# Decoder layer on one core: the normalized tokens of the self attention turned by way of memory and VectorE instead of by TensorE

## The chip, the core and the metric

One core of a Trainium2 chip runs the whole layer as one program. Time is microseconds of the device from start to end. The kernel before was run three times (3795.72, 3797.68 and 3800.22 us; the median is 3797.68), and once more with the hardware profiler, which gave the profile that all durations below come from.

## What is computed

The input is 32 sequences (called batches here) of 128 tokens with 512 channels, in fp32. Three blocks follow one another, each as `x = x + block(layernorm(x))`: a differential self attention, a cross attention and a mixture of experts. The change touches the first:

```python
h = (x - mean) / sqrt(var + 1e-5)            # per token
q, k, v = h @ Wq * 0.25, h @ Wk, h @ Wv      # 32 half heads of 16, 16 value heads of 32
aw = softmax(q @ k.T + causal)               # per half head
attn = (aw[0] - lam * aw[1]) @ v             # the two half heads of one head
attn = 0.2 * attn-normalized per head        # (1 - LAMBDA_INIT)
x = x + attn @ Wo
```

`h @ W` sums over channels, and TensorE sums over partitions. A batch arrives with tokens on the partitions, so `h` has to be turned (channels on the partitions, four chunks of 128) before it can be multiplied. How it is turned is what is changed.

## The kernel before, in words

`self_attention` runs over 64 steps, two for each batch `b`: step `n = 2b + cp` works on half `cp` of the channels of `q` and `k` (16 half heads). The work of one step is spread over several turns of the loop in lines 478 to 524 (the first lines of the loop are in `at`: the step that came `ago` turns earlier). Turn `n` issues, in this order: `turn_maxima` and half of the exponentials with their sums (`sums`, L278, ScalarE) for the step before; `maxima` for its own step (scores L251 on TensorE, mask L257 and row maxima L264 on VectorE); `queries_and_keys` (L220) for the next pair of batches, a quarter in each turn; `exponentials` (L308, L315, L318) and the other half of `sums` for the step before; `weigh` (L333, L337, L339) for the step two before; and then either `values` of the next pair (L238, odd turns) or `leave`, the product with Wo (L405, even turns).

Batches go in pairs (`G = 2`): projections are made for a pair, and `hT[g]` holds the turned tokens of pair `g`. Four turns of the loop make up a pair. The tokens of pair `g + 2` are prepared while the attention of pair `g` runs: `measure` (L56 to L66, mean and 1/deviation) in even turns, and in the odd turn behind it `normalize` (L87 on ScalarE: one pass over 128x512), `turn_in` and `load`, which asks for the next batch but one (L151).

`turn_in` is four transposes on TensorE into a PSUM tile (`turn4`, L95) and a copy of that tile by ScalarE into `hT` (L207). The loop calls it for batches 4 to 31, 28 in all; batches 0 to 3 are turned before the loop.

Two things set the order around this. The engines' queues: each engine runs its instructions in the order that the scheduler gave them (outside of the blocks under `manual_schedule`, where the program order holds; `issue_after` puts instructions behind a given one on its engine). And PSUM: every product asks for a tile of two banks from one pool of four (`banks`, `bufs=4`), so that the fourth request after one gets its tile again and has to wait until the earlier one was read out. A turn of the loop makes eight such requests, in program order `turn_maxima`, `maxima` (two), `queries_and_keys`, `exponentials` (two), `weigh`, and `values` or `leave`; an odd turn with `turn_in` makes a ninth.

After the first pair is under way the stage overlaps at its end with the cross attention (`beside`, from turn 60).

Of the kernel before, what the change touches and what calls it, by code (L numbers as in the profile page):

```python
# [10 lines left out]
F32 = mybir.dt.float32  # L11
# [7 lines left out]
P = 128  # L19
E = 512  # L20
EC = E // P
# [14 lines left out]
class Common:  # L36
# [49 lines left out]

        self.nc.scalar.activation(out, src, AF.Identity, bias=down, scale=rstd)  # L87

    def turn4(self, src, order=range(EC)):


        tr = self.banks()[:, 0, :].rearrange("p (c x) -> p c x", c=EC)
        cols = src.rearrange("p (c x) -> p c x", c=EC)
        for c, n in enumerate(order):
            self.nc.tensor.transpose(tr[:, c, :], cols[:, n, :], self.ident)  # L95
        return tr
# [15 lines left out]
            call(*args)  # L112


def self_attention(cm, x, x1_d, Wq, Wk, Wv, Wo, lq1, lk1, lq2, lk2, heads, heads_in, beside):

# [11 lines left out]
    nc, tc, bank = cm.nc, cm.tc, cm.banks  # L130
    B = x.shape[0]
    H, D, G = 16, 32, 2
    CP = 2
    ROW = (16, 0)
    with ExitStack() as ctx:
# [7 lines left out]
        pj2 = early.enter_context(tc.tile_pool(name="a_pj2", bufs=2))  # L143

        xin, xres = {}, {}

        def load(b, queue=nc.sync):

            if b < B:
                xin[b] = pj2.tile([P, E], F32, name="xin")  # L150
                queue.dma_start(out=xin[b], in_=x[b])  # L151
# [10 lines left out]
        for b in range(G):  # L162
            load(b, both[b % 2])
        w = {
            name: (wp if name == "wo" else pj).tile([P, EC, E], F32, name=name)
            for name in ("wk", "wq", "wv", "wo")
        }
        for oc in range(EC):
            for name, src, queue in (("wk", Wk, nc.sync), ("wq", Wq, both[oc < 2])):
                queue.dma_start(  # L170
                    out=w[name][:, :, ts(oc, P)],
                    in_=src[:, ts(oc, P)].rearrange("(c p) m -> p c m", p=P),
                )
            if oc == 0:
                nc.sync.dma_start(out=heads, in_=heads_in)
        vecs = wp.tile([P, 4, 16], F32, name="lam_vecs")
        for i, src in enumerate((lq1, lq2, lk1, lk2)):
            nc.sync.dma_start(out=vecs[:, i, :], in_=src.partition_broadcast(P))
        for name, src in (("wv", Wv), ("wo", Wo)):
            nc.sync.dma_start(out=w[name], in_=src.rearrange("(c p) m -> p c m", p=P))  # L180

        begun = wp.tile([P, 1], F32, name="a_begun")
        nc.scalar.activation(begun, cm.mhalf[:, 0:1], AF.Exp)
# [1 line left out]
        hT, qT, kz, k1, vs = {}, {}, {}, {}, {}  # L185
        last, last_v = {}, [None]
        h, sc_of, qm, expd, u, o, an = {}, {}, {}, {}, {}, {}, {}

        def measure(b):
            if b < B:  # L190
                h[b] = cm.moments(pj2, xin[b], "a_")

        def normalize(b):
            if b < B:
                rstd, down = h[b]
                h[b] = pj2.tile([P, E], F32, name="h")
                cm.shifted(h[b], xin.pop(b), rstd, down)

        def turn_in(b):

            if b >= B:
                return
            g, i = divmod(b, G)
            if i == 0:
                hT[g] = pj2.tile([P, EC, G * P], F32, name="hT")
            tr = cm.turn4(h.pop(b))
            nc.scalar.copy(hT[g][:, :, ts(i, P)], tr)  # L207

        def queries_and_keys(g, oc):

# [220 lines left out]
        for b in range(G):  # L431
# [8 lines left out]
            out=causal, in_=causal, compare_op=ALU.is_ge, fill=NEG, base=0,  # L440
# [32 lines left out]
        for b in range(G):  # L473
            turn_in(G + b)
            load(2 * G + b)
        first.close()
        steps = [(b, cp) for b in range(B) for cp in range(EC // CP)]
        for n in range(len(steps) + 5):
            g, k = divmod(n, 2 * G)
            if n == len(steps) - 2 * G:  # L480
                early.close()
            at = {ago: steps[n - ago] for ago in range(6) if 0 <= n - ago < len(steps)}
            if 1 in at:
                turn_maxima(*at[1])
                sums(*at[1], 0)
            if 0 in at:
                maxima(*at[0])
            queries_and_keys(g + 1, k)
            if 1 in at:
                exponentials(*at[1])  # L490
                sums(*at[1], 1)
            if 2 in at:
                weigh(*at[2])
            if k % 2:
                values(g + 1, k // 2)
            elif 5 in at:
                leave(at[5][0])
            if 2 in at:
                divide(*at[2])
                if at[2][1]:  # L500
                    finish(at[2][0])

            def behind():

                return tc.issue_after(last[at[0]].ins) if 0 in at else nullcontext()

            b = (g + 2) * G + k // 2
            if k % 2 == 0:
                if 3 in at:
                    with behind():  # L510
                        norms(at[3][0])
                measure(b)
                if 4 in at:
                    load_again(at[4][0])
            else:
                normalize(b)
                turn_in(b)
                load(b + G)
                if 4 in at:
                    with behind():  # L520
                        scale_out(at[4][0])
                    turn_out(at[4][0])
            if n in beside:
                beside[n]()


class CrossAttention:
# [101 lines left out]
    def load(self, b):  # L629
        src = self.src  # L630
        src[b, "k"] = self.pi.tile([P, E], F32, name="cx")
        self.nc.sync.dma_start(out=src[b, "k"], in_=self.ctx_in[b])
        src[b, "q"] = self.pi.tile([P, E], F32, name="h2")
        self.nc.sync.dma_start(out=src[b, "q"], in_=self.x1_d[b])

    def measure(self, b):
        q = self.sided[b, "q", 0] = self.pi.tile([P, E], F32, name="xq0", bufs=2)
        self.scale[b] = self.cm.moments_by_sums(self.pi, self.src[b, "q"], q, "x_")
# [575 lines left out]
class Shared:  # L1214
# [4 lines left out]
    G = 4  # L1219
# [482 lines left out]
def decoder_kernel(  # L1702
# [5 lines left out]
    nc = tc.nc  # L1708
# [15 lines left out]
    half_eid = const.tile([P, 2], I32, name="half_eid")  # L1724

    x1_d = dram.tile([B, P, E], F32, name="x1_d")
    h3_d = dram.tile([T, E], F32, name="h3_d")
    h3T_d = dram.tile([B, P, EC, P], F32, name="h3T_d")
    table_ds = [dram.tile([(NX * B + 2) * P, 2], F32, name=f"table_d{i}") for i in range(2)]
# [6 lines left out]
    with tc.tile_pool(name="x_w", bufs=1, side="right") as x_w:  # L1736
        rest = x_w.tile([P, E], F32, name="rest")
        nc.gpsimd.memset(rest, 0.0)
        routing = Routing(cm, x_w, table_ds, B)
        cross = CrossAttention(cm, x_w, x1_d, x2_d, h3_d, h3T_d, ctx_in, routing)  # L1740
        cross.plan(lambda: s_w.load(), lambda: shared.load(0))
        x_ctx = ExitStack()

        def begin():
            cross.begin(
                x_ctx.enter_context(
                    tc.tile_pool(name="x_in", bufs=2, side="right", reuse_waits="tile")
                )
            )
            cross.advance(7)  # L1750

        n = 2 * B
        beside = {
            12: lambda: cross.load_weights(
                xWq, xbq, xWk, xbk, xWv, xbv, xWo, xbo, cos, sin, rotT, gate_w
            ),
            20: lambda: cross.prepare(heads),
            28: routing.prepare,
            n - 4: begin,
        }  # L1760

        for i, count in enumerate((4, 4, 5, 2, 2, 2, 2)):
            beside[n - 3 + i] = lambda count=count: cross.advance(count)
        self_attention(cm, x, x1_d, aWq, aWk, aWv, aWo, lq1, lk1, lq2, lk2, heads, heads_in, beside)
        s_w_pool = ctx.enter_context(tc.tile_pool(name="s_w", bufs=1, reuse_waits="tile"))
        s_w = SharedWeights(cm, s_w_pool, sw_gate, sw_up, sw_down)
        s_h_pool = ctx.enter_context(tc.tile_pool(name="s_h", bufs=2, reuse_waits="tile"))
        shared = Shared(cm, s_h_pool, h3T_d, sum_d, out)
        x_out = ExitStack()
        p2 = x_out.enter_context(tc.tile_pool(name="x_p2", bufs=2, reuse_waits="tile"))  # L1770
        cross.run(p2)
        x_ctx.close()
        s_pool = x_out.enter_context(tc.tile_pool(name="s_p", bufs=1, reuse_waits="tile"))
        shared.use(s_pool, s_w)
        en = mybir.EngineType
        in_order = {en.PE, en.DVE, en.Activation, en.Pool}
        todo = [lambda: cross.rest(2)] * 34 + [
            lambda: routing.tiles(eid, fresh, rows, used, usual, mixed),
            lambda: routing.halves(half, half_eid),
            lambda: nc.sync.dma_start(out=sum_d[T : T + P, :], in_=rest),  # L1780
        ]

        def between():
            if todo:
                todo.pop(0)()

        EARLY = 3  # L1790
        with tc.manual_schedule(engines=in_order):
            for g in range(EARLY - 1):
                shared.group(g, False, between)
            while todo:
                between()
# [103 lines left out]
```

## Time and profile before

| | us |
|---|---|
| three runs, median (lowest to highest) | 3797.68 (3795.72 to 3800.22) |
| the profiled execution | 3800.08 |
| its span, from first to last instruction | 3798.3 |
| TensorE busy in the span | 3717.0 |
| VectorE, ScalarE, GpSimd busy | 2677.8, 2076.4, 1917.2 |
| from 104.37 to 652.9 us, the steady part of the self attention (548.53 us): TensorE, ScalarE, VectorE, GpSimd busy | 547.11, 497.91, 457.85, 282.95 |
| mean granted TensorE clock, share of full | 0.992 |

The self attention has about the first 790 us of the span, the last 75 of them beside the cross attention. In the profile PE is the matmul side of TensorE, PEld its weight loads, DVE VectorE, ACT ScalarE, POOL GpSimd and SPq the queue of SyncE, which issues nearly all of the DMAs. A row of the timeline has the start, the duration, the engine, the line of the kernel, the operation with output and inputs, and in brackets the idle time before it with what ended it. A row with `x16` merges sixteen instructions.

### The profile page before, as it was taken

Reading aid. Unit: us, or ns where it says so; the run is one execution under the profiler, and the core shown is the slowest. Engines: PE = TensorE matmul, PEld = TensorE weight load, DVE = VectorE, ACT = ScalarE, POOL = GpSimd, SP = SyncE. Lnnn points to the kernel's source line nnn. Section 1 sums busy time; section 2 is a strip of 40 time slices with the busy share of each in tenths; the row PEclk is TensorE's granted clock in tenths of the full one; section 3 lists DMA queues with packets and bytes.
Section 4 is the critical chain, followed back from the end, with each engine's and each line's share of the span. In section 5 each row is a group of like instructions: output and inputs, shape, how many; then the busy total and the mean of one; then the engine's idle time right before and its main releaser. Section 6 shows DMA issues by size and latency. Waiting matters only on the chain. (4 is left out here: it accounts for less than half of the span.)

```text
span 3798.3 us, 59896 instructions
## 1 busy us (share of the span) xinstructions
PE 3717.0 (98%) x19060; PEld 1967.8 (52%) x19060; DVE 2677.8 (70%) x5402; ACT 2076.4 (55%) x5616; POOL 1917.2 (50%) x2154
## 2 busy tenths in 40 slices
PE   8999999899999999999999999999999999999999
PEld 5666666534444444444445555555555555555444
DVE  4888888877777778787326777777777777776111
ACT  6989998847677676776402444444444444443000
POOL 3555455545777777777424554555555555553000
PEclk9999999999999999999999999999999999999999
DMA  3111110121221111111135565656566665564210
GB/s 113 34 35 35 35 37 30 39 83 49 62 60 42 51 51 51 48 49 40 56 110 169 128 164 134 166 121 164 122 156 142 150 150 141 135 172 81 89 56 33
DMA packets 146548, 340.25 MB, mean 90 GB/s; under 512 B 28976, under 2 KB 33776, under 8 KB 146160
## 3 DMA queue, kind: packets, MB, share of 16 engines
q1 hardware_dynamic: 89408, 227.75, 18.8%
q0 software_dynamic: 55616, 107.79, 15.4%
q8 instruction: 154, 2.52, 0.3%
q14 instruction: 170, 1.39, 0.1%
q10 hardware_dynamic: 1200, 0.79, 0.1%
HBM read 574.59 MB, written 102.17 MB: 178 GB/s over the span
## 5 line engine op out<-in xcount | busy, mean ns | idle before, releaser
L694 DVE TENSOR_REDUCE nm<-ps 128x2 f32<-128x1024 f32 x512 | 610.6, 1214 | 113.2 <-PE ps L690 106.8
L717 ACT ACTIVATE xp<-ps 128x1024 f32<-128x1024 f32 x512 | 505.8, 1021 | 264.5 <-PE ps L690 202.7
L1644 POOL DMA_INDIRECT sum_d<-e_out,e_into x192 | 309.9, 1614 | 562.6 <-ACT e_out L1641 438.4
L713 PE MATMUL ps<-xqn,xk 32*128 32x512 f32 x2048 | 528.9, 621 | 20.7 <-ACT xp L717 19.1
L1637 PE MATMUL ps<-wd,e_guT 128*128 128x512 f32 (+1 forms) x1152 | 526.9, 593 | 0.3 <-ACT e_guT L1627 0.3
L690 PE MATMUL ps<-xk,xq 32*128 32x512 f32 x2048 | 526.9, 631 | 0.1
L1584 DVE STREAM_TRANSPOSE e_xT<-e_xr 64x256 f32<-64x256 f32 x800 | 499.5, 624 | 18.9 <-DMA e_xr<-h_d,e_run_of 10.7
L1609 DVE STREAM_TRANSPOSE e_guT<-e_gu 32x96 f32<-32x96 f32 x1600 | 477.7, 299 | 25.2
L1569 POOL DMA_INDIRECT e_xr<-h_d,e_run_of x400 | 413.8, 1035 | 159.7 <-issue 150.0
L1598 PE MATMUL ps<-wg,e_xT 128*128 128x352 f32 x1536 | 486.7, 459 | 0.0
L1598 PE MATMUL ps<-wu,e_xT 128*128 128x352 f32 x1536 | 485.7, 459 | 0.0
L1627 ACT COPY e_guT<-e_turned 32x96 f32<-32x96 f32 (+1 forms) x1600 | 407.1, 254 | 25.1 <-DVE e_turned L1620 3.9
L1598 PEld LDWEIGHTS ps<-wg,e_xT 128*128 128x128 f32 x1536 | 289.7, 189 | 217.8 <-issue 94.5
L278 ACT ACTIVATE s<-s,a_nm 128x128 f32<-128x128 f32 x1024 | 395.7, 396 | 5.2 <-DVE a_nm L264 5.2
L1598 PEld LDWEIGHTS ps<-wu,e_xT 128*128 128x128 f32 x1536 | 291.8, 190 | 162.6
L1641 ACT ACTIVATE e_out<-ps,e_weight 128x512 f32<-128x512 f32 x200 | 137.4, 687 | 411.8 <-PE ps L1637 409.5
L1637 PEld LDWEIGHTS ps<-wd,e_guT 128*128 128x128 f32 (+1 forms) x1152 | 218.5, 190 | 228.2 <-issue 188.5
L1602 ACT ACTIVATE e_act<-ps 128x352 f32<-128x352 f32 x200 | 92.6, 463 | 412.7 <-PE ps L1598 412.7
L713 PEld LDWEIGHTS ps<-xqn,xk 32*128 32x128 f32 x2048 | 169.0, 184 | 285.5 <-ACT xp L717 124.5
L1603 DVE TENSOR_TENSOR e_gu<-e_act,ps 128x352 f32<-128x352 f32 x200 | 104.1, 521 | 274.6 <-ACT e_act L1602 274.1
L728 PE MATMUL ps<-xp,v 128*32 128x512 f32 x2048 | 233.0, 595 | 7.9 <-ACT xp L717 7.9
L1031 POOL DMA_INDIRECT table_d<-entry,at x192 | 202.4, 1054 | 64.0 <-issue 52.9
(310 smaller groups left out, 5575.4 us busy)
## 6 DMA issues: line engine op xcount, KB each, us to landing
wg<-in_L_ffn_w_gate_dram SPq DMA_DIRECT2D x192, 704.0 KB
wu<-in_L_ffn_w_up_dram SPq DMA_DIRECT2D x192, 704.0 KB
wd<-in_L_ffn_w_down_dram SPq DMA_DIRECT2D x192, 576.0 KB
wd<-in_L_ffn_w_down_dram SPq DMA_DIRECT2D x192, 128.0 KB
xg<-in_L_ffn_w_gate_dram SPq DMA_DIRECT2D x16, 704.0 KB
xu<-in_L_ffn_w_up_dram SPq DMA_DIRECT2D x16, 704.0 KB
xd<-in_L_ffn_w_down_dram SPq DMA_DIRECT2D x16, 576.0 KB
xres<-in_x_dram SPq DMA_DIRECT2D x32, 256.0 KB
```

The source lines that it names most:

```text
L278: nc.scalar.activation(s[:, j, c, side, :], s[:, j, c, side, :], AF.Exp, bias=nm[n][:, side, at : at + 1], accum_out=sm[n][:, to : to + 1],)
L690: self.nc.tensor.matmul(sc[:, i, :], q[rows, ts(c, P)], k[rows, :], start=True, stop=True)
L694: self.nc.vector.tensor_reduce(at[:, self.ROW[side], 2 * pair : 2 * pair + 2], sc, AX.X, ALU.max, negate=True)
L713: self.nc.tensor.matmul(sc[:, i, :], k[rows, ts(c, P)], q[rows, :], start=True, stop=True)
L717: self.nc.scalar.activation(e, sc, AF.Exp)
L1569: self.cm.nc.gpsimd.indirect_dma_start(out=xr[:, t, :], out_offset=None, in_=self.h3_d.rearrange("t (h f) -> (t h) f", h=self.R), in_offse ...
L1584: self.cm.nc.vector.transpose(to[ts(w, half), :, v], xr[ts(v, half), w])
L1598: nc.tensor.matmul(pgu[lanes, half, 0:M], t[:, c, lanes], w[:, c, :], start=c == 0, stop=c == EC - 1,)
L1609: self.cm.nc.vector.transpose(t[ts(q, 32), :, ts(s, 32)], self.part(q, 3)[ts(s, 32)])
L1627: self.cm.nc.scalar.copy(t[ts(q, 32), 0:n, ts(s, 32)], z[ts(s, 32), q - half, 0:n])
L1637: nc.tensor.matmul(py[lanes], t[:n, c, lanes], wd[:n, c, :], start=c == 0, stop=c == last)
L1644: nc.gpsimd.indirect_dma_start(out=self.sum_d[:, :], out_offset=bass.IndirectOffsetOnAxis(ap=into, axis=0), in_=y[:, :], in_offset=None, b ...
```

## The change

Batches 0 to 3 are turned as before, but by strided columns: chunk `c` now holds channels 4j + c in place of 128c + j, and the rows of Wk, Wq and Wv are loaded in that order (`(p c)` in place of `(c p)`). For the other 28, `normalize` and `turn_in` give way to `send` in the even turn and `receive` in the odd one. `send` normalizes with ScalarE, which now writes each 128 channels as 4 runs of 32 (its innermost step in the output is 32 elements); one DMA writes the 256 KB to a DRAM buffer, and four DMAs, one for each group of 32 partitions, read it back in runs of 512 bytes. `receive` is one VectorE transpose of 128x512 in blocks of 32x32, into `hT`. PSUM and TensorE have no part in it. `send` and `receive` are traced under `behind()`, which puts what they have on VectorE behind the row maxima of their own turn; `measure` now comes one batch ahead, in the same even turn, and `load` too is called there. The copy L207 is left out with the transposes.

```diff
-    def turn4(self, src, order=range(EC)):
+    def turn4(self, src, order=range(EC), strided=False):
-        cols = src.rearrange("p (c x) -> p c x", c=EC)
+        cols = src.rearrange("p (x c) -> p c x" if strided else "p (c x) -> p c x", c=EC)
...
-                    in_=src[:, ts(oc, P)].rearrange("(c p) m -> p c m", p=P),
+                    in_=src[:, ts(oc, P)].rearrange("(p c) m -> p c m", p=P),
...
-            tr = cm.turn4(h.pop(b))
-            nc.scalar.copy(hT[g][:, :, ts(i, P)], tr)
+        def turn_in(b):
+            nc.scalar.copy(turned(b), cm.turn4(h.pop(b), strided=True))
+
+        def send(b):
+            if b >= B:
+                return
+            rstd, down = h[b]
+            t = pj2.tile([P, E], F32, name="h")
+            cm.shifted(
+                t.rearrange("p (q c f) -> p q f c", q=4, c=EC),
+                xin.pop(b).rearrange("p (q f c) -> p q f c", q=4, c=EC), rstd, down,
+            )
+            nc.sync.dma_start(out=h_d[b], in_=t)
+            h[b] = pj2.tile([P, 4, P], F32, name="h_runs")
+            for q in range(4):
+                nc.sync.dma_start(
+                    out=h[b][ts(q, 32)],
+                    in_=h_d[b][:, ts(q, P)].rearrange("(t i) r -> i t r", i=32),
+                )
+
+        def receive(b):
+            if b < B:
+                nc.vector.transpose(
+                    turned(b).rearrange("p c (t i) -> p c t i", i=32),
+                    h.pop(b).rearrange("p t (c f) -> p c t f", c=EC),
+                )
...
+        measure(2 * G)
         first.close()
...
-                measure(b)
+                with behind():
+                    send(b)
+                    measure(b + 1)
+                load(b + G)
                 if 4 in at:
                     load_again(at[4][0])
             else:
-                normalize(b)
-                turn_in(b)
-                load(b + G)
+                with behind():
+                    receive(b)
```

More of the change, by code (lines that the diff above doesn't have):

```diff
@@ L112, in run, with self_attention @@
             call(*args)
-def self_attention(cm, x, x1_d, Wq, Wk, Wv, Wo, lq1, lk1, lq2, lk2, heads, heads_in, beside):
+def self_attention(cm, x, x1_d, h_d, Wq, Wk, Wv, Wo, lq1, lk1, lq2, lk2, heads, heads_in, beside):
     nc, tc, bank = cm.nc, cm.tc, cm.banks
@@ L178, in self_attention @@
             nc.sync.dma_start(out=vecs[:, i, :], in_=src.partition_broadcast(P))
-        for name, src in (("wv", Wv), ("wo", Wo)):
-            nc.sync.dma_start(out=w[name], in_=src.rearrange("(c p) m -> p c m", p=P))
+        nc.sync.dma_start(out=w["wv"], in_=Wv.rearrange("(p c) m -> p c m", p=P))
+        nc.sync.dma_start(out=w["wo"], in_=Wo.rearrange("(c p) m -> p c m", p=P))
         begun = wp.tile([P, 1], F32, name="a_begun")
@@ L197, in normalize, with turned @@
                 cm.shifted(h[b], xin.pop(b), rstd, down)
-        def turn_in(b):
-            if b >= B:
-                return
+        def turned(b):
             g, i = divmod(b, G)
@@ L205, in turn_in @@
                 hT[g] = pj2.tile([P, EC, G * P], F32, name="hT")
-            tr = cm.turn4(h.pop(b))
-            nc.scalar.copy(hT[g][:, :, ts(i, P)], tr)
+            return hT[g][:, :, ts(i, P)]
+        def turn_in(b):
[22 more added lines that the diff above has]
+                )
         def queries_and_keys(g, oc):
@@ L1726, in decoder_kernel @@
     x1_d = dram.tile([B, P, E], F32, name="x1_d")
+    h_d = dram.tile([B, P, E], F32, name="h_d")
     h3_d = dram.tile([T, E], F32, name="h3_d")
@@ L1763, in decoder_kernel @@
             beside[n - 3 + i] = lambda count=count: cross.advance(count)
-        self_attention(cm, x, x1_d, aWq, aWk, aWv, aWo, lq1, lk1, lq2, lk2, heads, heads_in, beside)
+        self_attention(cm, x, x1_d, h_d, aWq, aWk, aWv, aWo, lq1, lk1, lq2, lk2, heads, heads_in, beside)
         s_w_pool = ctx.enter_context(tc.tile_pool(name="s_w", bufs=1, reuse_waits="tile"))
```

## The prediction, made before the changed kernel was run

> **What bounds the kernel now.** I read the busy times by stretch first, to find the limit of the stage that the change touches; then the timeline of one batch, to see what TensorE does in it; then the same timeline a little later, where the loop still runs but has no batch left to turn.
>
> Busy time by stretch (start:end, length, then PE, PEld, DVE, ACT, POOL with their instruction counts, granted clock, DMA share, GB/s):
>
> ```profile
> 400.68:423.26 22.58, 22.58 (x189) 14.44 (x187) 18.87 (x28) 20.55 (x80) 12.00 (x13) 1.00 0.11 36
> 682.99:704.50 21.51, 21.51 (x183) 13.72 (x182) 18.14 (x25) 19.36 (x78) 10.89 (x11) 1.00 0.08 27
> ```
>
> The first line is one batch (two turns of the loop) of the steady part: PE is never idle, ACT has 2.0 us left, DVE 3.7. The second is a batch late in the loop, without `normalize`, `turn_in` and `measure`: PE is still never idle, but the batch takes 21.51 us. So TensorE sets the pace, and it has 1.07 us less to do, or to wait for, without the turn.
>
> The timeline around the end of an odd turn and the start of an even one, steady part:
>
> ```profile
> 399.81 0.59 PE L238 MATMUL ps<-wv,hT 128*128 128x512 f32 x1
> ...
> 400.24 0.60 PE L95 MATMUL ps<-ident,h 128*128 128x128 f32 x4
> ...
> 400.68 0.38 PE L291 MATMUL ps<-ident,a_nm 128*128 128x128 f32 x2
> ...
> 400.99 1.80 PE L251 MATMUL ps<-kz,qT 32*128 32x256 f32 x16
> 401.03 0.57 ACT L242 COPY v<-ps 128x512 f32<-128x512 f32 x1
> ...
> 401.65 0.73 PEld L251 LDWEIGHTS ps<-kz,qT 32*128 32x128 f32 x12 [0.36 <-ACT v L242]
> 402.03 0.57 ACT L207 COPY hT<-ps 128x512 f32<-128x512 f32 x1
> ...
> 402.71 1.59 PEld L220 LDWEIGHTS ps<-hT,wk 128*128 128x128 f32 x8 [0.33 <-ACT hT L207]
> 402.72 1.99 PE L220 MATMUL ps<-hT,wk 128*128 128x256 f32 x8
> ```
>
> Two costs show. The four transposes push L291 from 400.24 to 400.68: 0.44 us. And L251, which takes 1.07 us to the next product in the other turn (412.39 to 413.46), takes 1.73 here (400.99 to 402.72): after four of its sixteen products it waits for the copy of `v` (L242). "PE busy" hides that, since ends are modelled. The reason is the ring of four PSUM tiles: the ninth request of the odd turn shifts it by one, so that the second half of the scores gets the tile that `values` has just filled. The same place in the later batch:
>
> ```profile
> 693.74 0.38 PE L291 MATMUL ps<-ident,a_nm 128*128 128x128 f32 x2
> 694.05 1.15 PE L251 MATMUL ps<-kz,qT 32*128 32x256 f32 x16
> ...
> 694.52 0.57 ACT L242 COPY v<-ps 128x512 f32<-128x512 f32 x1
> ...
> 695.14 1.59 PEld L220 LDWEIGHTS ps<-hT,wk 128*128 128x128 f32 x8 [0.35 <-ACT v L242]
> 695.15 1.99 PE L220 MATMUL ps<-hT,wk 128*128 128x256 f32 x8
> ```
>
> With eight requests in each turn the tile of `v` falls to L220, which is 1.10 us after L251; L242 ends at 695.09, just in time.
>
> **What goes.** Per batch, PE loses 0.44 us of transposes and 0.66 us of waiting (1.73 - 1.07), and 0.03 come back as the wait of L220 (1.10 - 1.07): 1.07 us, the difference of the two periods. ACT loses L207 (0.57 us). What is late next is L242 to L220, a chain through ACT that has no slack left; whatever I add to ACT between the end of L220 in an odd turn and L242 lengthens the period one for one.
>
> The loop turns 28 batches. The first falls in the start (turn 1), where PE waits for ACT anyway (L251 at 60 us waits 1.7 us for L242); I count it at nothing. 27 x 1.07 = **28.9 us**.
>
> **What is added or moved, and what hides it.**
>
> ACT: in the changed kernel's compiled order, `send`'s L87 stands in the even turn between the copy of `qT` (L231) and the exponentials (L315); `normalize` stood in the same turn ahead of L226. In the later batch, which has no L87 at all, ACT waits in the odd turn for L220, and DVE waits at the even turn's start for L291:
>
> ```profile
> 688.13 0.84 ACT L226 ACTIVATE kz<-ps,a_keep 128x256 f32<-128x256 f32 x2 [1.57 <-PE ps L220]
> 694.15 0.87 DVE L293 SCALAR_TENSOR_TENSOR qm<-qT,a_others,ps 128x256 f32<-128x256 f32 x2 [0.95 <-PE ps L291]
> ```
>
> So an L87 of up to 1.57 us delays nothing that PE waits for. At its old 0.82 us (L87 at 405.20) it is free. But it now writes with a step of 128 bytes from element to element, which no row of ACT shows. Lower end 0.82 (the same elements); upper end 1.59, as if each quarter cost as much as a 128x128 L278 (4 x 0.397, by its mean). Both are hidden, but for 0.02. I take 0.82. Cover gone, each further microsecond costs 27.
>
> DVE: `receive` is compiled behind L264 of the odd turn, ahead of L384, L392 and L339. The nearest row is L392, a transpose of the same 128x512: 0.71 us. The other end is L1584, which reads with a step of four elements: 0.62 for 64x256, so 1.25 for twice the columns. DVE has 0.95 us before L293 and 0.27 more before L257 (its mask waits for PE at 695.30), so both ends are hidden; I take 0.71. Behind it stand L384, L392, L339, L348 and L352; the one that PE needs soon is L339, which empties the tile that the second half of L251 takes now: it ends 3.2 us ahead of that (691.38 against 694.6), and comes 0.71 later. `measure` one batch ahead takes away DVE's wait for the load (L56, 0.78 us at 408.61); DVE has that to spare, so nothing is gained.
>
> DMA: five more issues per batch on SP (0.33 us each, as L151 has them). The way from L87 to `receive`: the store lands 2.03 us after its issue (L398 at 415.02 waits for the store at 412.99); the load of `xin` queued behind the store is issued meanwhile; four loads 4 x 0.33; the last lands 2.57 after its issue (L151 at 406.04, L56 at 408.61): 5.9 us. In the later batch's clock, L87 would end at 700.83 and L264 of the next odd turn at 710.82: 10.0 us. So the data is there 4.1 us early. Behind the waiting SP queue stand the store of x1 (L410) and the load of `xres` (L398), both needed a whole batch later. Traffic rises by 512 KB a batch, 24 GB/s over the 36 of the first line; the DMA engines are at 0.11.
>
> Start: sixteen transposes now read with a step of 16 bytes (upper end: twice the 1.11 us that four take at 12.34, on the path for two groups, 2.2 us; lower end nothing), and one L87 (0.82) moves into a stretch where ACT is the bound, against a L207 (0.58) that leaves it. I take 1 us lost. The wider weight rows cost nothing: the first L220 waits for L207, not for weights.
>
> Sum: 28.9 - 1 = 28 us. The profiled execution was 3800.1 (span 3798.3 and 1.8 around it): 3772. It lay 2.4 above the median of 3797.7, so for the median **3770 us**.
>
> The Trainium skill, on the page "SBUF — State Buffer", section "Door 1: The DMA port swizzle", speaks against the new L87: lines of 16 bytes, and a penalty for each access that goes to a new one, with no figure. L1584 and L392 fit it (2.4 ns a column with a 16-byte step, 1.4 without). L87 slowed in that ratio would be 1.44 us, an estimate, and still be hidden. The page "VectorE: DVE Perf Modes", "Rules for kernel authors", would leave a 128x128 transpose on TensorE if PSUM will do. By price that holds here too (0.44 us on PE and 0.57 on ACT against 0.71 on DVE and five DMAs); the sum goes the other way only because PE is the engine without slack.
>
> **Rivals.**
>
> *Part of it comes back* (17%). L87 above 1.57 us, or `receive` with its followers late enough that POOL's L363 and then ACT's L368 slip, so that ACT takes over as the bound. For it: ACT has 20.55 of 22.58 us now, and would have 20.0 of 21.5. Against: the 1.57 above. L87 at 2.0 would cost 0.43 x 27 = 12 us: 3782. Range 3773 to 3790.
>
> *The turn was never in the way* (8%). If the modelled PE time misleads and the later batch is faster because ACT and DVE have less to do there (19.36 for 20.55), the period stays: 3798. Against: the shifted L291 and the wait for L242 are times of starts.
>
> *The way by memory is too long* (15%), slower. DVE stops at `receive` until the last of the four loads has landed. DVE has 1.66 us of slack a batch (21.51 - 18.14 - 0.71, and 1.0 for `measure`'s three instructions), so from 10.0 + 1.7 = 11.7 us on the period grows, and from 12.7 it is longer than today. If the loads of 512-byte runs went one after the other at 3.6 us each (the longest wait of L398 for a store), the way would be 2.0 + 14.4 = 16.4, the period 21.5 + 4.7 = 26.2 and the kernel 27 x 3.6 = 98 us slower: 3896. For it: no row has such loads in the steady part. Against: the DMA engines are nearly idle.
>
> **How the numbers follow.** Forecast 60% (3766 to 3773), partial 17%, no change 8%, slower 15%. The 8-in-10 range takes the forecast with its ends (2.2 us more in the start, or nothing) and the partial case: 3765 to 3792. About 0.2%, 7.6 us, is what a measurement of this kernel can tell from no change: faster 0.77, same 0.08, slower 0.15.
>
> **What would show it.** In the profile after: 21.5 us from the L291 of one even turn to that of the next; L251 1.07 us to its follower in both turns; L220's weight load with a wait of some 0.35 for the copy of `v`; L87 under 1.6 us; `receive` near 0.7 us without a DMA wait. Wrong would be DVE idle for `h_runs`, ACT without idle time ahead of L226, or a batch that still takes 22.6.

## The result, and the profile after

The changed kernel takes 3896.54 us (median of four runs, 3895.78 to 3897.95); the kernel before, on the same chip, 3797.44 (3795.72 to 3800.22). The ratio is 1.026, with a 95% interval of 1.0248 to 1.0272. The prediction was 3770, so it missed by 127 us and had the wrong sign.

Line numbers have moved: L251 of before is now L277, L291 is L317, L315 is L341, L220 is L246, L242 is L268, L405 is L431. The new `receive` is L230, the store of `send` L219, its four loads L222.

The top of the page after:

```profile
span 3896.1 us, 59916 instructions
...
PE 3734.5 (96%) x18948; PEld 1970.2 (51%) x18948; DVE 2697.5 (69%) x5430; ACT 2073.1 (53%) x5588; POOL 1914.9 (49%) x2154
...
PEclk9899999999999999999999999999999999999999
```

TensorE has 112 instructions less and is yet busy for 17.5 us longer (3734.5 for 3717.0), with idle time on top. The three batches that answer to the 22.58 us of before, by the same columns (start:end, length, PE, PEld, DVE, ACT, POOL, granted clock, DMA share, GB/s):

```profile
393.80:421.32 27.52, 24.59 (x182) 15.38 (x182) 19.69 (x29) 20.47 (x78) 11.42 (x12) 0.88 0.16 48
421.32:446.67 25.35, 22.10 (x182) 13.72 (x182) 19.96 (x29) 20.27 (x78) 12.04 (x12) 1.00 0.18 53
446.67:473.29 26.62, 23.44 (x182) 14.70 (x182) 19.92 (x29) 20.46 (x78) 11.91 (x12) 0.94 0.16 51
```

No engine is busy for the whole batch any more. PE, never idle before, stands for 3 us of every batch, and in two batches of the three its granted clock is down as well. What PE waits for, from the waits between 100 and 640 us (engine, tile and line, what it waited for: us in total, times, longest):

```profile
ACT h L87 <- POOL a_ln_down L66: 100.5, 20, 5.2
...
PE ps L317 <- ACT e L341: 48.2, 19, 2.7
...
PE ps L277 <- ACT e L341: 14.2, 20, 5.9
```

ScalarE stops at `send`'s L87 for 5.0 us a batch, until GpSimd has made the mean's term (L66). One such stop in the timeline:

```profile
414.44 0.38 ACT L257 ACTIVATE qT<-ps 128x256 f32<-128x256 f32 x1
420.03 1.26 ACT L87 ACTIVATE h<-xin,a_ln_down,a_ln_rstd 128x512 f32<-128x512 f32 x1 [5.21 <-POOL a_ln_down L66]
421.10 1.95 ACT L341 ACTIVATE e<-ps 128x1024 f32<-128x1024 f32 x2
```

Between the copy of `qT` (L257) and the exponentials (L341) ScalarE does nothing but wait for L87's operand. On TensorE the same moment looks like this:

```profile
415.88 3.60 PE L431 MATMUL ps<-wo,anT 128*128 128x512 f32 x8
422.20 0.44 PE L317 MATMUL ps<-ident,a_nm 128*128 128x128 f32 x2 [2.73 <-ACT e L341]
423.10 1.15 PE L277 MATMUL ps<-kz,qT 32*128 32x256 f32 x16 [0.46 <-ACT e L341]
```

The next turn's L317 needs a PSUM tile that L341 empties, and L341 is queued behind L87. And this is what ScalarE waits for, on VectorE and GpSimd:

```profile
415.36 0.68 DVE L56 BATCH_NORM_STATS2 a_ln_stats<-xin 128x6 f32<-128x512 f32 x1
...
416.20 2.92 POOL L404 TENSOR_TENSOR rr<-ms,mhalf 128x16 f32<-128x16 f32 x1 [0.82 <-DVE ms L402]
416.29 0.15 DVE L60 TENSOR_SCALAR a_ln_ve<-a_ln_mv 128x1 f32<-128x1 f32 x1
...
419.09 0.54 POOL L62 TENSOR_TENSOR a_ln_rstd<-a_ln_ve,mhalf 128x1 f32<-128x1 f32 x1
...
419.74 0.26 POOL L66 TENSOR_SCALAR a_ln_down<-a_ln_mv,a_ln_rstd 128x1 f32<-128x1 f32 x1
```

L56 to L66 is `measure`, and in this turn it measures the next batch (`measure(b + 1)` in the diff). So the L87 that waits for it is the `send` of the next batch, which the program calls two turns later. The scheduler has put that L87 a whole batch early. The whole trace agrees: the loop's third L87 stands in turn 2 (70.48 us), though `send` is called for it in turn 4, and behind the last L87 (735.40) two `receive`s follow (745.08 and 767.56), where the program has one. `behind()` did not hold it: it names an instruction of VectorE and binds what stands on VectorE. On ScalarE only the data bound L87, and they are there as soon as its own L66 is done. Before it, POOL works 2.92 us on the power of another batch's norms (L404).

The theory: the loss is this wait, ScalarE standing at an L87 that came into its queue too early; bound to its own step, the change would give what was predicted. The rivals: the way by memory is too long after all (the prediction's slower rival, priced at 3896); the strided write of L87 is the loss; the new order of `measure` gains or loses by itself. The price of the first rival and the measured time agree by chance: L230 never waited for its loads in the changed kernel.

### The profile page after: what moved, and what is told of

Its sections match the earlier page's. It is cut to its first block, busy times and chain, and to the rows that moved or that the text cites. A ratio compares the mean times of both kernels' runs of the same rounds, so it can differ in the third digit from the quotient of the medians.

```text
span 3896.1 us, 59916 instructions
## 1 busy us (share of the span) xinstructions
PE 3734.5 (96%) x18948; PEld 1970.2 (51%) x18948; DVE 2697.5 (69%) x5430; ACT 2073.1 (53%) x5588; POOL 1914.9 (49%) x2154
## 5 line engine op out<-in xcount | busy, mean ns | idle before, releaser
L253 POOL TENSOR_SCALAR k<-kz,a_keep,a_extra 128x256 f32<-128x256 f32 x128 | 78.1, 619 | 346.6 <-ACT kz L252 346.6
```

## The experiments

All are compared with the kernel before, run on the same chip.

**L87 bound to its own step.** In the changed kernel, `send`'s L87 is put behind the copy of `qT` of its turn, which stands on ScalarE.

```diff
-            cm.shifted(
...
+            with tc.issue_after(last_q[0].ins):
+                cm.shifted(
...
-            nc.scalar.mul(qT[g][:, oc], both[:, 1], 0.25)
+            last_q[0] = nc.scalar.mul(qT[g][:, oc], both[:, 1], 0.25)
```

> The changed kernel with one edge more: send's pass on ScalarE (L87) is put behind the copy of qT of its own turn on ScalarE, so that it can't be compiled two turns earlier. Wait theory (L87 of a batch was compiled into the turn in which VectorE and GpSimd only just work out its mean and deviation, and ScalarE stands there with the exponentials behind it): no wait of L87 for GpSimd, a batch takes 21.5 us at full clock, and the time falls by some 125 us against the changed kernel, to 3768 to 3775. Memory theory (the way by DRAM, five DMAs and the VectorE turn are too long or disturb the rest): stays within 20 us of 3896.

Measured: 3769.57 us (3766.53 to 3771.27), ratio 0.9927 (0.991 to 0.9943). It beats both kernels. A batch, and the stretch around L87:

```profile
415.43:436.93 21.50, 21.50 (x183) 13.72 (x183) 18.90 (x30) 20.39 (x78) 11.51 (x12) 1.00 0.21 63
```

```profile
413.81 0.39 ACT L258 ACTIVATE qT<-ps 128x256 f32<-128x256 f32 x1
414.08 1.32 ACT L87 ACTIVATE h<-xin,a_ln_down,a_ln_rstd 128x512 f32<-128x512 f32 x1
415.16 2.01 ACT L342 ACTIVATE e<-ps 128x1024 f32<-128x1024 f32 x2
...
418.68 0.38 PE L318 MATMUL ps<-ident,a_nm 128*128 128x128 f32 x2
419.10 0.26 POOL L66 TENSOR_SCALAR a_ln_down<-a_ln_mv,a_ln_rstd 128x1 f32<-128x1 f32 x1
...
424.92 0.70 DVE L231 STREAM_TRANSPOSE hT<-h_runs 128x512 f32<-128x512 f32 x1
```

L87 stands in the same place between L258 and L342, and waits for nothing: its L66 is that of the turn two before. The L66 of this turn comes 5 us later and holds nobody. PE has no idle time in the batch, and `receive` (L231) has no wait. This one binding is worth 127 us.

**The new order without the way by memory.** In the kernel before, with its transposes on TensorE, only the order is made like the changed kernel's.

```diff
+        measure(2 * G)
...
-                measure(b)
+                with behind():
+                    normalize(b)
+                    measure(b + 1)
+                load(b + G)
...
-                normalize(b)
                 turn_in(b)
-                load(b + G)
```

> The kernel before with the new order alone: normalize in the even turn with measure one batch ahead and load behind it; the turn stays on TensorE, no DRAM, no strided write. Wait theory: ScalarE waits for GpSimd ahead of L87 here too, a batch takes 25 to 26 us and the whole 3880 to 3910. Memory theory: as before, 3790 to 3800.

Measured: 3911.04 us, ratio 1.0301 (1.0284 to 1.0318); the waits between 100 and 640 us, and one L87:

```profile
ACT h L87 <- POOL a_ln_down L66: 101.6, 21, 4.8
```

```profile
343.21 0.81 ACT L87 ACTIVATE h<-xin,a_ln_down,a_ln_rstd 128x512 f32<-128x512 f32 x1 [4.84 <-POOL a_ln_down L66]
```

The same wait, and a loss of the same kind (1 us above the range that I gave), with not a byte more through memory and no strided write. The way by memory isn't needed for the loss.

**The new order, with L87 bound.** The same, with L87 behind the copy of `qT` as in the first experiment (for the batches of the loop).

```diff
-                cm.shifted(h[b], xin.pop(b), rstd, down)
+                with tc.issue_after(last_q[0].ins) if b >= 2 * G else nullcontext():
+                    cm.shifted(h[b], xin.pop(b), rstd, down)
```

> The kernel before with the new order of normalize, measure and load, L87 bound behind the copy of qT of its own turn, and the turn still on TensorE. It parts the order from the way by memory. If what the change brings is the work taken from TensorE and the ninth request to the PSUM ring, this stays at the time of before: 3793 to 3802, 27 or 28 us above the bound kernel. If the gain of the bound kernel came from the order, this would be near 3770 too.

Measured: 3795.64 us, ratio 0.9996 (0.9986 to 1.0006), one batch:

```profile
400.00:422.58 22.58, 22.58 (x189) 14.44 (x188) 18.88 (x28) 20.45 (x80) 12.04 (x13) 1.00 0.11 36
```

22.58, as before. So the order gives nothing by itself, and the gain of the first experiment (22.58 to 21.50) is what leaving TensorE brings.

**A shorter wait.** In the changed kernel, `send` and `measure` are traced ahead of `norms`, and the power L404 is put behind L66 on POOL; L87 stays early.

```diff
-        nc.gpsimd.tensor_scalar(down, mv[:, 0:1], rstd, -1.0, ALU.mult, ALU.mult)
+        self.last_down = nc.gpsimd.tensor_scalar(down, mv[:, 0:1], rstd, -1.0, ALU.mult, ALU.mult)
...
-            nc.gpsimd.tensor_tensor(rr, ms, cm.mhalf, ALU.pow)
+            with tc.issue_after(cm.last_down.ins):
+                nc.gpsimd.tensor_tensor(rr, ms, cm.mhalf, ALU.pow)
```

> The changed kernel with measure's two GpSimd instructions (L62, L66) put ahead of the power of norms (2.92 us) on GpSimd, by tracing measure first and an edge; L87 is still compiled a batch early. Wait theory: L87's wait shrinks from some 5 to some 2.5 us, TensorE's stall at the next turn's start nearly goes, a batch takes 22.3 to 23 us, the whole 3785 to 3815. Memory theory: stays within 20 us of 3896.

Measured: 3801.68 us, ratio 1.0015 (1.0005 to 1.0025), inside what was expected:

```profile
323.36 1.29 ACT L87 ACTIVATE h<-xin,a_ln_down,a_ln_rstd 128x512 f32<-128x512 f32 x1 [1.71 <-POOL a_ln_down L66]
```

With the 2.92 us of L404 out of the way, the wait falls from 5.21 to 1.71 us here (from 5.0 to 1.8 on average between 100 and 640 us), and 95 of the 127 us come back. The time follows the length of this wait.

**L87 without its step**, once in the changed kernel and once with L87 bound. The output is then written in the input's order, so that the channels of 28 batches are mixed up further on.

```diff
-            cm.shifted(
-                t.rearrange("p (q c f) -> p q f c", q=4, c=EC),
-                xin.pop(b).rearrange("p (q f c) -> p q f c", q=4, c=EC), rstd, down,
-            )
+            cm.shifted(t, xin.pop(b), rstd, down)
```

> The changed kernel with L87 writing its columns in order, without the runs of 32, so that channels are mixed up in the products (the values differ, the amount of work does not). Price of the strided write: L87 falls from 1.26 to 0.82 us; as ScalarE is what TensorE waits for, 27 x 0.44 = 12 us less than the changed kernel, 3884. If the strided write were the main cause, it would be back near 3797.

> The changed kernel with L87 bound to its own turn, and with its columns written in order (channels are mixed up in the products; the amount of work is the same). If the slower strided pass (1.3 in place of 0.8 us) is hidden once ScalarE doesn't wait, this lies within 3 us of the bound kernel, 3770. If ScalarE were still part of the bound there, it would be up to 12 us faster, 3758.

Measured: 3882.2 us (3875.83 to 3892.02; ratio 1.0235, 1.0215 to 1.0254) in the changed kernel, 14 less, for an L87 of 0.81 instead of 1.26. That would fit a pass that costs what it lasts when it stands on the path (0.45 x 27 = 12), but the four runs spread over 16 us and the interval touches that of the changed kernel, so this price is not shown. L87 still waits 4.9 us a batch. With L87 bound 3766.46 (0.9918, 0.9902 to 0.9935), against 3769.57 with the step; the intervals overlap. There no price of the step can be told from noise, as foretold. It is no rival for 127 us.

**More work for TensorE.** `leave`'s product with Wo (L431) is made twice for 24 batches, once in the changed kernel and once with L87 bound.

```diff
-            for c in range(EC):
+            for c in list(range(EC)) * (2 if b < 24 else 1):
```

> The changed kernel as it is, but the product with Wo (L431) is made twice for 24 batches, the first pass being overwritten: 1.7 us more work on TensorE per batch, right before the place where it waits 2.7 us for ScalarE. If TensorE's lower granted clock in this stage (0.94 in most batches, which take 26.6 us in place of 25.3) comes from its idle time, the clock rises and the kernel gets faster in spite of more work: down by 15 to 30 us, 3865 to 3880. If the clock has another cause, the products fill idle time and the kernel stays within 6 us of 3896.

> Control for the run with the doubled product: the same doubling in the bound kernel, where TensorE has no idle time. 24 x 1.72 = 41 us slower than the bound kernel: 3811, less up to 6 us if some of it fits into waits.

Measured: the changed kernel becomes **faster** with the added work, 3875.28 us (ratio 1.0207, 1.019 to 1.0224), 21 less. Two of its batches:

```profile
408.27:433.93 25.66, 25.30 (x192) 15.40 (x191) 19.34 (x29) 20.28 (x78) 11.91 (x12) 1.00 0.17 52
433.93:459.29 25.36, 24.70 (x191) 15.10 (x190) 19.58 (x29) 20.27 (x78) 11.84 (x12) 1.00 0.18 53
```

The period is about the 25.35 of the changed kernel's batch at full clock, and the clock is 1.00 in each batch from 126 to 714 us. The added product fills the time in which PE waited for ScalarE: L317 has no wait left. With L87 bound, where PE has no such time, the same product costs 80.5 us (3850.05; ratio 1.0141, 1.0124 to 1.0158). I had expected half of that, since I counted the product as four instructions of 0.43 us; it is eight of them. (The first of the two runs fell inside its range with twice the work that I had reckoned with.) In the kernel before the product takes 3.44 us (408.64 to 412.08), and 24 x 3.44 = 83. So the control costs its full price, and in the changed kernel the same work costs less than nothing.

**A longer way by memory**, with L87 bound: two, and then four, copies from DRAM to DRAM between the store and the four loads. The data are the same.

```diff
-            nc.sync.dma_start(out=h_d[b], in_=t)
+            nc.sync.dma_start(out=way[0][b], in_=t)
+            for k in range(2):
+                nc.sync.dma_start(out=way[k + 1][b], in_=way[k][b])
...
-                    in_=h_d[b][:, ts(q, P)].rearrange("(t i) r -> i t r", i=32),
+                    in_=way[-1][b][:, ts(q, P)].rearrange("(t i) r -> i t r", i=32),
```

> The bound kernel with the way by memory made longer: the normalized tokens are copied twice more from DRAM to DRAM (two DMAs of 256 KB, each behind the one before) before they are read back. In the bound kernel the store is issued at 415.43 us and the VectorE turn stands at its place 9.5 us later, with the data there after some 6. Two copies of 2 to 2.6 us make the way 10 to 11 us; VectorE has 1.7 us a batch to spare, so nothing or little is lost: 3768 to 3785.

> The same with four copies more: a way of 14 to 16.5 us against the 11.2 that are free. If the slower rival of the prediction is priced rightly, the period grows by what lies beyond, 3 to 5 us a batch: 3850 to 3910. If it stays under 3790, the way has more room than the prediction gave it.

Measured: 3818.4 us (3810.82 to 3825.79; ratio 1.0061, 1.0045 to 1.0078) and 3956.91 (1.0419, 1.0402 to 1.0437). Both miss what I expected, upward. The first in the timeline, SyncE's queue and VectorE:

```profile
414.51 0.34 SPq L221 DMA_DIRECT2D h_d<-h  x1
417.15 3.33 SPq L223 DMA_DIRECT2D h_d<-h_d  x2
423.31 1.75 SPq L226 DMA_DIRECT2D h_runs<-h_d  x4
...
427.57 0.71 DVE L234 STREAM_TRANSPOSE hT<-h_runs 128x512 f32<-128x512 f32 x1 [4.33 <-DMA h_runs<-h_d]
```

From the store's issue at 414.51 to the transpose at 427.57 it takes 13.1 us: a copy holds the way for some 3.1 us, more than I had allowed, and VectorE now waits 3.4 us on average (1.6 to 4.3 between 100 and 640 us). With four copies the way is 18.6 us, the wait 6.6 on average and the clock 0.90 to 0.92. This is the slower rival in the flesh, and the first run fits its threshold: the loss of 48.8 us is 1.8 us a batch, against a wait of 3.4 less the 1.7 of slack that VectorE was said to have. (With four copies the same sum gives 4.9 of the 6.9 us a batch; the clock is lower there too, and I have not parted the two.) But the rival shows as idle time of VectorE ahead of the transpose, and the changed kernel has none.

## Why the prediction was wrong

The step that failed is one sentence: "in the changed kernel's compiled order, `send`'s L87 stands in the even turn between the copy of `qT` (L231) and the exponentials (L315)". The place was right (the timeline has L87 there); the batch was not. I took that L87 for the one that the turn calls, whose mean and deviation had been ready for a batch. It is that of the next batch, one `measure` further on. So I costed a new place as a duration (0.82 us, hidden under 1.57) and no wait at all, where a wait of 5.0 us came with it, and with it the exponentials and the whole next turn behind L87 on ScalarE. Counting the L87s of the compiled order against the L66s would have told it. No rival of mine had this mechanism.

What the wait costs: a batch at full clock takes 25.35 us after, 21.50 with L87 bound; 27 x 3.85 = 104 us. The other 23 of the 127 are 0.85 us a batch, and go with the lower clock of batches such as the 27.52 and the 26.62. That split is worked out; that the idle time of PE costs clock is shown by the doubled product, which brought 21 of these 23 back.

The other terms, in the kernel with L87 bound, where they can be seen alone:

- *TensorE sets the pace, and a batch takes 21.51 us without the turn*: 21.50. In the turn behind `values` the scores (L278) have 1.10 us to their follower (408.23 to 409.33), where before they had 1.73, as the ring of PSUM tiles would have it; the changed kernel has 1.09 there (408.86 to 409.95). The wait that remains is the one foretold, 0.35 us for the copy of `v`, in the kernel with L87 bound:

```profile
408.23 1.15 PE L278 MATMUL ps<-kz,qT 32*128 32x256 f32 x16
409.32 1.59 PEld L247 LDWEIGHTS ps<-hT,wk 128*128 128x128 f32 x8 [0.35 <-ACT v L269]
```

- *28 us in sum, 3770*: 3769.57. With 27 x 1.08 = 29.2 less the 27.3 measured, 1.9 us are left for the start, where I took 1; I have not measured it by itself.
- *L87 0.82, bounds to 1.59*: 1.26 to 1.32, near the upper end, and hidden where nothing waits ahead of it. The bounds held; the value that I took did not. The Trainium skill, page "SBUF — State Buffer", section "Door 1: The DMA port swizzle", gives the rule for lines of 16 bytes and no figure; the measured price of a step of 128 bytes on this pass is 0.45 to 0.51 us over 0.81.
- *`receive` 0.71*: 0.70, hidden.
- *The way by memory 5.9 us, 10.0 to be had*: the issues of the loads begin 2.01 us after the store's (415.43, 417.44) with L87 bound, and with the 4.26 us from there to the transpose that the longer way shows (423.31 to 427.57) the sum is some 6.3, of 9.5 (415.43 to 424.92). The rival "too long" is refuted for the changed kernel, and its 12.7 us fit the longer way, which at 13.1 us is slower than the kernel before (3818.4 for 3797.36).
- *The turn was never in the way*: refuted by the 0.9927.

## What to carry to other kernels

A compiled order tells where an instruction stands, not whose it is: before its place is costed, count the instances up to it against the instances that it depends on. The order edges of this kernel bound only on the engine of the instruction that they name, so a chain over several engines needs one on each, above all on the engine whose queue holds others up. An early instruction is no gain when its operand comes late: on an in-order engine its wait is everybody's wait.

## What the runs showed of the hardware

The granted clock of TensorE falls to half, and stays there after the idle time is over. Two gaps of the changed kernel are alike: TensorE waits 2.71 us for L341 before 394.68, and 2.73 us before 422.20. Three stretches of 1 us behind the first (columns as in the table of batches):

```profile
394.80:395.80 1.00, 0.79 (x6) 0.39 (x10) 0.40 (x1) 1.00 (x3) 1.00 (x2) 0.50 0.98 250
...
399.80:400.80 1.00, 1.00 (x4) 0.73 (x4) 0.96 (x2) 1.00 (x6) 0.00 (x0) 0.50 0.00 0
...
401.80:402.80 1.00, 1.00 (x6) 0.63 (x4) 1.00 (x2) 0.00 (x0) 0.00 (x0) 1.00 0.06 21
```

After the first gap TensorE ran at half its clock for some 6 us of full work, and only then at 1.00. After the second it ran at 1.00 throughout (the batch of 25.35). The batch so struck is 27.52 - 25.35 = 2.17 us longer. The Trainium skill, page "TensorE: Matmul & The Clock Gate", section "HAM oscillation — how this bites in real kernels", tells of this half clock after gaps of over some 3.4 us. The halving agrees; the size of gap doesn't. The ends of products are modelled, and counted between the weight loads the two gaps are 3.54 and 3.55 us, but a wait of 2.03 us before 447.55 (2.86 between the weight loads) was also followed by 3 us at 0.50. And of two equal gaps only one was. Where TensorE waits, added work can therefore make a kernel faster: 21 us in the changed kernel. A ScalarE pass over 128x512 takes 0.81 us into consecutive elements and 1.26 to 1.32 with 128 bytes from one to the next.
